# Projecting q with its head columns on partitions, rope pairs as block rows, and weights prepared in half-size units

## The chip, the core and the metric

The kernel runs on one core of a Trainium2 chip. The time is the device time of one execution in microseconds (us); three executions of the kernel before are shown. Everything is computed in float32. A core has a matrix engine (TensorE, PE in the profile), a vector engine (VectorE, DVE), a scalar engine (ScalarE, ACT) and GpSimd (POOL), each running its own instructions in order, and SyncE (SP), which here issues most of the DMA transfers. SBUF is the memory on the chip, with 128 partitions; PSUM holds what TensorE writes, in banks of 512 numbers a partition.

## The reference

One layer of linear attention and one sparse gated feed-forward network, each between a layer norm and a residual. Cut to what matters:

```python
def attention(x, Wq, Wk, Wv, Wo):          # x: (2, 1024, 512); 16 heads of q, 4 of k and v, 128 wide
    q = (x @ Wq.T) ; k = (x @ Wk.T) ; v = (x @ Wv.T)      # split into heads
    q = q * cos + rotate_half(q) * sin     # rope: element d is paired with d + 64 of its head
    k = k * cos + rotate_half(k) * sin
    qf, kf = elu(q) + 1, elu(k) + 1        # four heads of q share one head of k and v
    for each token s: state += kf_s v_s^T ; z += kf_s ; out_s = (qf_s state) / (qf_s z + 1e-6)
    return out @ Wo.T

def ffn(x, w_gate, w_up, w_down):          # 2048 wide
    h = silu(x @ w_gate) * (x @ w_up)
    return keep_2_largest_of_4(h) @ w_down

x = x + layernorm(attention(layernorm(x), ...))
x = x + layernorm(ffn(layernorm(x), ...))
```

## The kernel before, in words

**Strassen products.** All large matrix products are made by one scheme, `strassen` (L109 to L146): the product of two 2x2 block matrices in 7 block products instead of 8, run in the order 1, 2, 6, 5, 7, 4, 3. Each operand comes as seven "factors" (four blocks or their sums; `FACTORS` says which go together). The sums between products are kept apart by PSUM copies on ACT (`keep`, L120) and by additions on DVE (L129, L139, L145); product 7 is added into the bank of which product 6's copy must be done, and so on. Product 4 ends block c21 (handed to `done`), product 3, the last, block c12. `step_input` (L545) makes x's factors from transposed x, `sums` (L412) those of the weights.

**Attention** runs in 16 steps n = 0 to 15: gp = n // 8 is a pass over half of the heads (8 of q, 2 of k and v), c = n % 8 a chunk of 128 tokens of both batches. A step works on the products of k and v (`kv_products`, L611) and of q (`q_products`, L634) for step n + 1, on the four groups of step n, and on the output product of step n - 1 (`o_products`, L747). A group i is one batch and one head of k with its four heads of q:

- `features` (L584): on DVE u = q cos (L592) and r = the rotated half times sin (L598, L599), on POOL u + r (L600), on ACT a relu and an exp (L602, L603), on DVE one last operation (L604). Tokens lie on partitions here, so the rope pair lies within a row. For q's four groups this comes after product 2, at product 4, after product 7's addition and after product 3.
- `q_transposed` (L663): four transposes on TensorE (`transposed`, L528: PSUM pool of two buffers), then an ACT copy to SBUF (L665). `k_transposed` (L629) does the same for k's four.
- `scores` (L668): kT times qT, masked by DVE into `am` (L679).
- `attend` (L684): per head of q one matmul with the state (L697) and one with `am` (L698), of 129 columns (the last column sums z); then, on DVE, the denominators (L703, L704) and o (L706), and the new state (L716, L718).
- `o_transposed` (L733): four transposes of o, an ACT copy for groups 0 to 2 (L738), and for the last group the sums that make the other factors (L741 to L745, one of them on POOL).

A group of q is `(b, j)`, batch and head of k, from `GROUPS` (L609).

**Order.** TensorE's, POOL's and SP's orders are written out by hand (`tc.manual_schedule`, L803); those of DVE and ACT are chosen by a scheduler when the kernel is built, but for the first lines. In each step `first(i)` (L830) issues the transposes ahead of group i, `second(i)` (L844) its attention and the scores of the next; between them parts of the three Strassen runs are advanced, so that TensorE has work while the other engines prepare.

**Start.** The kernel loads x(0), the weights of k and v, of q (L431, in four quarters of 512 columns, 2 KB rows), the rope table (L433), x(1), wo's, x(2), on the queues of ACT and SP. kv(0) and q(0) (the products of step 0) run before any group.

**Weights of later work** are "prepared" by the generator `prepare` (L446): 17 units, each loaded to SBUF (L443), summed by POOL (four operations, L461 to L465) and stored to DRAM as factors (L457, L469). Each call of `first` advances it once; ahead of the units it makes wo's sums (`prepare_all`, L508).

**FFN.** Four blocks of 512 tokens (`hidden` L265, `down` L314) of Strassen products (L218, L324), with the selection of 2 of 4 on DVE and POOL. The first gate products are interleaved with the last attention step.

Of the kernel before, what the change touches and what calls it, by code (L numbers as in the profile page):

```python
# [35 lines left out]
def kernel(  # L36
# [366 lines left out]
    def q_quarter(gp, i, k):  # L403
        return rows(wq, 2 * k, 2, (2 * gp + i) * 512, 512)
# [7 lines left out]
    def sums(t, engine):  # L412
        a11, a12, a22, s2, s4, s3, s1 = (t[:, i] for i in range(7))
        for o, i0, i1, op in (
            (s1, s3, a22, ALU.add),
            (s3, a11, s3, ALU.subtract),
            (s2, s1, a11, ALU.subtract),
            (s4, a12, s2, ALU.subtract),
        ):
            engine.tensor_tensor(o, i0, i1, op)  # L420
            yield

    def load_quarters(t, quarter, engines):
# [7 lines left out]
    load_quarters(wq_sb, q_quarter, (nc.scalar, nc.sync))  # L431
# [5 lines left out]
    xt[2] = load_x(2)  # L437
    weights = {0: (wkv_sb, wq_sb, wo_sb)}

    def prepare_load(src, view, dst):  # L440
        q = prep.tile([P, 4, 512], F32, tag="q", name="wraw")
        for to, of in src(q):
            nc.sync.dma_start(out=to, in_=of)  # L443
        return view(q), dst
# [29 lines left out]
    def whole(of):  # L474
        return lambda q: [(q, of)]

    def quarters(quarter, part):
        def src(q):
            for n, (i, k) in enumerate(((0, 0), (0, 1), (1, 0), (1, 1))):
                of = quarter(1, i, k)[:, part]  # L480
                yield q[:, n, :].rearrange("p (k c) -> p k c", c=of.shape[2]), of

        return src

    def view_quarters(q):
        return [q[:, n, :] for n in range(4)]

    def view_gu(q):
        v = q.rearrange("p (h k) (j m c) -> p h k j m c", h=2, j=2, m=2)
        return [v[:, h, :, :, m, :] for m, h in ((0, 0), (0, 1), (1, 0), (1, 1))]  # L490

    def view_d(q):
        v = q.rearrange("p (h k) (m c) -> p h k m c", h=2, m=2)
        return [v[:, h, :, m, :] for m, h in ((0, 0), (0, 1), (1, 0), (1, 1))]

    def into_gu(t):
        return lambda n: t[:, n, :].rearrange("p (k j c) -> p k j c", k=2, j=2)

    def into_d(jb):
        return lambda n: d_dram[:, n, jb, :].rearrange("p (k c) -> p k c", k=2)  # L500

    def into_part(t, part):
        return lambda n: t[:, n, part]

    def part_of(t, part):
        return lambda n: t[:, n, part].rearrange("p k c -> p (k c)")

    def prepare_all():  # L508
        yield from sums(wo_sb, nc.gpsimd)
        units = []  # L510
        for quarter, t, parts in (
            (kv_quarter, wkv_dram, (slice(0, 2),)),
            (q_quarter, wq_dram, (slice(0, 1), slice(1, 2))),
            (o_quarter, wo_dram, (slice(0, 2), slice(2, 4))),
        ):
            for part in parts:
                units.append((quarters(quarter, part), view_quarters, part_of(t, part)))
        for jb in range(NJB):
            for i, w in enumerate((w_gate, w_up)):
                units.append((whole(columns(w, jb)), view_gu, into_gu(gu_dram[jb][i])))  # L520
        for jb in range(NJB):
            of = w_down[jb * 512 : (jb + 1) * 512, :].rearrange("(p r) o -> p r o", r=4)
            units.append((whole(of), view_d, into_d(jb)))
# [56 lines left out]

    def strassen_a(width, product, c11, c12, c22, done):
        return strassen((ps_mm, qp), [P, width // HD, HD], product, c11, c12, c22, done)

    def features(src, c, dst):  # L584
# [5 lines left out]
        u = rawp.tile([P, 4, HD], F32, tag="u", name="u")  # L590
        r = rawp.tile([P, 4, HD], F32, tag="r", name="r")
# [13 lines left out]

    kf, kT, v1, qf = {}, {}, {}, {}
    GROUPS = ((0, 0), (1, 1), (0, 1), (1, 0))  # L609
# [24 lines left out]
    def q_products(n):  # L634
        c = n % NC
        raw = [rawp.tile([P, REP, HD], F32, tag="raw", name="qraw", bufs=4) for _ in range(3)]

        def feature(i, src):
            f = qp.tile([P, REP, HD], F32, tag="qf", name="qf", bufs=3)
            features(src, c, f)  # L640
            qf[n, i] = f

        run = strassen_a(
            512,
            project(weights[n // NC][1], xf[n]),
            raw[0],
            raw[2],
            raw[1],
            lambda t: feature(2, t),
        )  # L650
        for i, _ in enumerate(run):
            if i == 1:
                feature(0, raw[0])
            elif i == 4:
                feature(1, raw[1])
            elif i == 6:
                feature(3, raw[2])
            yield

    state = {}  # L660
    qT, am, o = {}, {}, {}

    def q_transposed(n, i):  # L663
        t = qp.tile([P, REP, P], F32, tag="qT", name="qT")
        nc.scalar.copy(t, transposed(qf.pop((n, i))))  # L665
        qT[n, i] = t

    def scores(n, i):  # L668
# [5 lines left out]
            qT[n, i].rearrange("p h t -> p (h t)"),  # L674
# [9 lines left out]
    def attend(n, i):  # L684
# [8 lines left out]
        q, a = qT.pop((n, i)), am.pop((n, i))  # L693
        for h in range(REP):
            dst = nmv[:, h // 2, h % 2, :]
            if c > 0:
                nc.tensor.matmul(dst, q[:, h, :], state[b, j], start=True, stop=False)  # L697
# [35 lines left out]
    def o_transposed(n, i):  # L733

        t = transposed(o.pop((n, i)))
        if i < 3:
            place = (0, 2, 1)[i]
            nc.scalar.copy(factor(n, place, 1 if place == 1 else 2), t)  # L738
# [271 lines left out]
```

## Time and profile before

| | |
|---|---|
| median of three executions | 1396.29 us (1395.09, 1396.29, 1398.87) |
| the profiled execution | 1395.51 us |
| its span, first to last instruction | 1393.8 us |
| mean granted TensorE clock | 0.996 |
| first kv product, first q product | 18.9 us, 29.9 us |
| last q product of attention ends, first FFN product starts | 724 us, 772 us |
| DMA: 109732 packets, 197.48 MB | mean 142 GB/s |

The profile comes from a hardware profiler during one execution, so rows are durations in that execution. A row of its groups names the line of the kernel, the engine, the operation, output and input by the program's names, the shape (partitions x elements) and the number; then the total busy time, the mean of one in ns, and the idle time of the engine just before those instructions with what ended it. A row of a timeline gives the start in us, the duration, the engine, line, operation and shape, and in brackets the wait before it and its releaser. A row of the windows gives the stretch, then for PE, weight loads, DVE, ACT and POOL the busy time and the number of instructions, then the granted clock, the DMA share and GB/s. Digits of the slices are busy tenths of 40 equal parts of the span.

### The profile page before, as it was taken

To read this page: it belongs to the slowest core of one execution; us is meant where nothing else is said; L and a number is where in the kernel's file an instruction comes from. 1 tells how busy PE (TensorE), PEld (TensorE's weight loads), DVE (VectorE), ACT (ScalarE), POOL (GpSimd) and SP (SyncE) were. 2 spreads that over 40 slices of the span, in tenths; PEclk is the share of its full clock that TensorE was granted. 3 is DMA by queue.
4 is the path that set the end of the run, shared out by engine and by line. 5 is a ranking of instruction groups with operands and counts; after the bars stand their busy time and mean duration, and the time that the engine had idled before them with its cause. 6 is when DMAs were issued, how large, how long until landed. Compare 5 with 4: busy or idle time off the path is not lost. (4 is left out here: it accounts for less than half of the span.)

```text
span 1393.8 us, 17195 instructions
## 1 busy us (share of the span) xinstructions
PE 1335.9 (96%) x6384; PEld 1069.0 (77%) x6384; DVE 835.1 (60%) x1570; ACT 447.3 (32%) x797; POOL 321.5 (23%) x259
## 2 busy tenths in 40 slices
PE   4899999999999999999999999999999999999997
PEld 2567778777876787667678888888888888888886
DVE  5785766564556565656566439816772577526852
ACT  1543433433233324333342323214330333113210
POOL 0333322332333343444332110100000100110001
PEclk9999999999999999999999999999999999999999
DMA  6131345035841736233443455346544655355321
GB/s 245 42 125 52 105 162 186 28 97 178 274 140 64 242 113 215 82 108 123 153 144 129 128 213 152 116 165 217 152 128 152 222 153 154 117 201 152 91 79 73
DMA packets 109732, 197.48 MB, mean 142 GB/s; under 512 B 8272, under 2 KB 51280, under 8 KB 105552
## 3 DMA queue, kind: packets, MB, share of 16 engines
q1 hardware_dynamic: 107520, 194.02, 43.1%
q10 hardware_dynamic: 2128, 2.36, 0.5%
q8 instruction: 51, 0.84, 0.2%
q14 instruction: 33, 0.27, 0.1%
HBM read 145.23 MB, written 51.12 MB: 141 GB/s over the span
## 5 line engine op out<-in xcount | busy, mean ns | idle before, releaser
L120 ACT COPY u<-cb 128x512 f32<-128x512 f32 (+1 forms) x252 | 126.1, 500 | 474.7 <-PE cb L218 183.1
L600 POOL TENSOR_TENSOR u<-u,r 128x512 f32<-128x512 f32 x80 | 101.8, 1273 | 300.9 <-DVE r L599 190.1
L570 PE MATMUL cb<-wq,xf 128*128 128x512 f32 x256 | 121.3, 596 | 7.0 <-ACT u L120 7.0
L755 PE MATMUL cb<-wo,of 128*128 128x256 f32 x512 | 121.2, 379 | 0.5 <-ACT u L120 0.5
L218 PE MATMUL cb<-fxt,wgu 128*128 128x256 f32 x512 | 117.8, 381 | 1.0 <-ACT u L120 1.0
L218 PE MATMUL cb<-fxnT,wgu 128*128 128x256 f32 x512 | 116.9, 379 | 0.0
L755 PEld LDWEIGHTS cb<-wo,of 128*128 128x128 f32 x512 | 95.9, 190 | 26.3 <-issue 11.9
L218 PEld LDWEIGHTS cb<-fxt,wgu 128*128 128x128 f32 x512 | 96.6, 190 | 16.4 <-ACT u L120 3.6
L218 PEld LDWEIGHTS cb<-fxnT,wgu 128*128 128x128 f32 x512 | 97.1, 190 | 13.8 <-issue 0.5
L604 DVE SCALAR_TENSOR_TENSOR qf<-u,r 128x512 f32<-128x512 f32 x64 | 65.4, 1021 | 66.3 <-ACT r L603 58.4
L168 POOL TENSOR_TENSOR h<-h 128x512 f32<-128x512 f32 x16 | 23.5, 1467 | 331.1 <-DVE ht L165 331.1
L602 ACT ACTIVATE r<-u 128x512 f32<-128x512 f32 x80 | 50.4, 631 | 153.9 <-POOL u L600 153.9
L139 DVE TENSOR_TENSOR y<-u,ce 128x256 f32<-128x256 f32 (+1 forms) x20 | 9.5, 474 | 146.8 <-ACT u L120 146.8
L698 PE MATMUL nm<-v,am 128*128 128x129 f32 x512 | 96.0, 277 | 1.5 <-DVE am L679 1.5
L570 PEld LDWEIGHTS cb<-wq,xf 128*128 128x128 f32 x256 | 46.6, 190 | 55.9 <-issue 40.7
L697 PE MATMUL nm<-state,qT 128*128 128x129 f32 x448 | 86.6, 275 | 0.0
L698 PEld LDWEIGHTS nm<-v,am 128*128 128x128 f32 x512 | 76.8, 194 | 3.4 <-issue 3.3
L697 PEld LDWEIGHTS nm<-state,qT 128*128 128x128 f32 x448 | 71.0, 191 | 7.7 <-issue 6.2
L570 PE MATMUL cb<-wkv,xf 128*128 128x256 f32 x256 | 67.8, 388 | 1.9 <-DVE xf L556 1.4
L671 PE MATMUL sc<-qT,kT 128*128 128x512 f32 x128 | 66.1, 598 | 0.0
L324 PE MATMUL cb<-wd,h 128*128 128x256 f32 x256 | 58.3, 381 | 4.0 <-DVE h L306 3.9
L755 PE MATMUL ce<-wo,of 128*128 128x256 f32 x256 | 60.5, 379 | 0.0
(151 smaller groups left out, 2571.6 us busy)
## 6 DMA issues: line engine op xcount, KB each, us to landing
wgu<-gs SPq DMA_DIRECT2D x112, 256.0 KB, 2.7
wgu<-us SPq DMA_DIRECT2D x112, 256.0 KB, 2.7
wd<-d_dram SPq DMA_DIRECT2D x28, 1024.0 KB, 4.8
xf<-xf SPq DMA_DIRECT2D x16, 896.0 KB, 5.1
x<-in_x_dram SPq DMA_DIRECT2D x16, 512.0 KB, 5.9
gs<-wraw SPq DMA_DIRECT2D x28, 256.0 KB, 3.5
us<-wraw SPq DMA_DIRECT2D x28, 256.0 KB, 3.5
d_dram<-wraw SPq DMA_DIRECT2D x28, 256.0 KB, 2.8
```

What stands on the lines that cost most here:

```text
L120: nc.scalar.copy(t, b)
L168: (engine or nc.gpsimd).tensor_tensor(b12, b22, b12, ALU.subtract)
L218: nc.tensor.matmul(bank[:, j, :], w[:, k, j, :], xf[xi][:, k, :], start=(start and j == 0 and k == 0), stop=(j == 1 and k == 1), skip_grou ...
L324: nc.tensor.matmul(bank[:, j, :], hf[jb][hi][:, k, j * P : (j + 1) * P], w[:, jb, k, :], start=(start and jb == 0 and j == 0 and k == 0), ...
L570: nc.tensor.matmul(bank.rearrange("p h d -> p (h d)"), x_[:, xi, k, :], w[:, wi, k, :], start=(start and k == 0), stop=(k == 1), skip_grou ...
L600: nc.gpsimd.tensor_tensor(u, u, r, ALU.add)
L602: nc.scalar.activation(r, u, AF.Relu, scale=-1.0)
L604: nc.vector.scalar_tensor_tensor(dst, u, 0.0, r, ALU.max, ALU.add)
L671: nc.tensor.matmul(sc.rearrange("p h t -> p (h t)"), kT[n][:, 2 * b + j, :], qT[n, i].rearrange("p h t -> p (h t)"), start=True, stop=True,)
L697: nc.tensor.matmul(dst, q[:, h, :], state[b, j], start=True, stop=False)
L698: nc.tensor.matmul(dst, a[:, h, :], v, start=(c == 0), stop=True)
L755: nc.tensor.matmul(bank.rearrange("p h d -> p (h d)"), of[n, xi][:, k, :], w[:, wi, k, :], start=(start and k == 0), stop=(k == 3), skip_g ...
```

## The change

q is projected with the operands of TensorE exchanged (`project_transposed`): the weights are held, 128 columns at a time, and x's transposed chunk is streamed, so that a product leaves the columns of heads on partitions and 128 tokens along the row, as the scores need them. The 2x2 blocks are now (halves of heads) x (batch): the first block row holds elements 0 to 63 of each of the eight heads, the second 64 to 127, and 128 partitions hold the halves of two heads. So the two members of a rope pair stand in the same place of two blocks, and both are needed before rope can start.

- `q_quarter` picks the interleaved halves of heads, 64 columns (256 B) at a time; the first load of wq becomes eight transfers.
- Rope for q works along tokens, so the tables are transposed once: `transpose_rope`, called between kv(0) and q(0), with four DVE copies, four sets of four transposes on TensorE and four ACT copies.
- `features_transposed` does a batch's two groups at a time: two halves, each with two DVE products, one POOL operation, two ACT operations and two final DVE operations of 64 partitions, which write the halves of a head onto the partitions 0 to 63 and 64 to 127 of `qT`. It is called at product 4 (batch 0) and after product 3 (batch 1). u and r have three buffers instead of two.
- `q_transposed` is gone, with its 64 sets of transposes and ACT copies.
- `GROUPS` goes batch by batch. In `o_transposed` two of the ACT copies remain, one group is written straight as a difference by DVE, and the last by DVE, ACT and POOL.
- The units of the weights that are prepared are half as wide: 34 instead of 17, and `second` advances the generator as well as `first`. wo's sums, ahead of the units, so come one per `first` or `second`.

The diff, cut to its core:

```diff
@@ -401,7 +401,9 @@
         return rows((wk, wv)[i], 2 * k, 2, gp * 256, 256)
     def q_quarter(gp, i, k):
-        return rows(wq, 2 * k, 2, (2 * gp + i) * 512, 512)
+        of = rows(wq, 2 * k, 2, 8 * gp * HD, 8 * HD)
+        return of.rearrange("p k (h i d) -> p k h i d", h=8, i=2)[:, :, :, i, :]
     def o_quarter(gp, i, k):
         return rows(wo, (2 * gp + k) * 4, 4, i * 256, 256)
...
-    load_quarters(wq_sb, q_quarter, (nc.scalar, nc.sync))
+    for k in range(2):
+        for n, (to, i, kh) in enumerate(((0, 0, 0), (1, 0, 1), (5, 1, 0), (2, 1, 1))):
+            (nc.scalar, nc.sync)[n % 2].dma_start(
+                out=wq_sb[:, to, k, :].rearrange("p (h d) -> p h d", h=8),
+                in_=q_quarter(0, i, kh)[:, k],
+            )
...
+    rope_T = [wp.tile([P, S], F32, name=name) for name in ("cos_T", "sin_T")]
+    def transpose_rope():
+        for t, k in zip(rope_T, (0, 2)):
+            for c in range(0, NC, 4):
+                twice = rawp.tile([P, 4, 2, 64], F32, tag="u", name="twice", bufs=3)
+                of = rope_sb[:, c : c + 4, k, :].unsqueeze(2).broadcast_to([P, 4, 2, 64])
+                nc.vector.tensor_copy(twice, of)
+                pt = transposed(twice.rearrange("p c s d -> p c (s d)"))
+                nc.scalar.copy(t[:, c * P : (c + 4) * P].rearrange("p (j t) -> p j t", j=4), pt)
...
-        q = prep.tile([P, 4, 512], F32, tag="q", name="wraw")
+        q = prep.tile([P, 4, 256], F32, tag="q", name="wraw")
...
+        yield from sums(all_of(wo_sb), nc.gpsimd)
+        units = [unit(kv_quarter, k, wkv_dram) for k in range(2)]
+        units += [unit_q(k, n) for k in range(2) for n in range(2)]
+        units += [unit(o_quarter, k, wo_dram) for k in range(4)]
...
+            units += [unit_gu(w, jb, i, j) for i, w in enumerate((w_gate, w_up)) for j in range(2)]
+        units += [unit_d(jb, k) for jb in range(NJB) for k in range(2)]
...
+    def project_transposed(w, x_):
+        def product(bank, i, start):
+            wi, xi = FACTORS[i]
+            for hp in range(4):
+                for k in range(2):
+                    nc.tensor.matmul(
+                        bank[:, hp, :],
+                        w[:, wi, k, hp * P : (hp + 1) * P],
+                        x_[:, xi, k, :],
+                        start=(start and hp == 0 and k == 0),
+                        stop=(hp == 3 and k == 1),
+                        skip_group_check=True,
+                    )
+        return product
...
-        u = rawp.tile([P, 4, HD], F32, tag="u", name="u")
-        r = rawp.tile([P, 4, HD], F32, tag="r", name="r")
+        u = rawp.tile([P, 4, HD], F32, tag="u", name="u", bufs=3)
+        r = rawp.tile([P, 4, HD], F32, tag="r", name="r", bufs=3)
...
+    def features_transposed(lo, hi, c):
+        cos, sin = (
+            t[:, c * P : (c + 1) * P].unsqueeze(1).broadcast_to([P, 4, P]) for t in rope_T
+        )
+        t = qp.tile([P, 4, 2, P], F32, tag="qT", name="qT")
+        for i, (same, other, op) in enumerate(((lo, hi, ALU.subtract), (hi, lo, ALU.add))):
+            u = rawp.tile([P, 4, P], F32, tag="u", name="u", bufs=3)
+            r = rawp.tile([P, 4, P], F32, tag="r", name="r", bufs=3)
+            nc.vector.tensor_tensor(u, same, cos, ALU.mult)
+            nc.vector.tensor_tensor(r, other, sin, ALU.mult)
+            nc.gpsimd.tensor_tensor(u, u, r, op)
+            nc.scalar.activation(r, u, AF.Relu, scale=-1.0)
+            nc.scalar.activation(r, r, AF.Exp, scale=-1.0)
+            for s in range(2):
+                half_of = slice(64 * s, 64 * s + 64)
+                nc.vector.scalar_tensor_tensor(
+                    t[64 * i : 64 * i + 64, :, s, :], u[half_of], 0.0, r[half_of], ALU.max, ALU.add
+                )
+        return t
+    kf, kT, v1, qT = {}, {}, {}, {}
+    GROUPS = ((0, 0), (0, 1), (1, 0), (1, 1))
...
-        raw = [rawp.tile([P, REP, HD], F32, tag="raw", name="qraw", bufs=4) for _ in range(3)]
-        def feature(i, src):
-            f = qp.tile([P, REP, HD], F32, tag="qf", name="qf", bufs=3)
-            features(src, c, f)
-            qf[n, i] = f
-        run = strassen_a(
-            512,
-            project(weights[n // NC][1], xf[n]),
-            raw[0],
-            raw[2],
-            raw[1],
-            lambda t: feature(2, t),
-        )
-        for i, _ in enumerate(run):
-            if i == 1:
-                feature(0, raw[0])
-            elif i == 4:
-                feature(1, raw[1])
-            elif i == 6:
-                feature(3, raw[2])
-            yield
+        raw = [rawp.tile([P, 4, P], F32, tag="raw", name="qraw", bufs=4) for _ in range(3)]
+        def done(hi):
+            qT[n, 0] = features_transposed(raw[0], hi, c)
+        yield from strassen_a(
+            512, project_transposed(weights[n // NC][1], xf[n]), raw[0], raw[1], raw[2], done
+        )
+        qT[n, 1] = features_transposed(raw[1], raw[2], c)
...
-    def q_transposed(n, i):
-        t = qp.tile([P, REP, P], F32, tag="qT", name="qT")
-        nc.scalar.copy(t, transposed(qf.pop((n, i))))
-        qT[n, i] = t
...
-            qT[n, i].rearrange("p h t -> p (h t)"),
+            qT[n, b][:, 2 * j : 2 * j + 2].rearrange("p a s t -> p (a s t)"),
...
-        q, a = qT.pop((n, i)), am.pop((n, i))
+        q, a = qT[n, b], am.pop((n, i))
...
-                nc.tensor.matmul(dst, q[:, h, :], state[b, j], start=True, stop=False)
+                nc.tensor.matmul(dst, q[:, 2 * j + h // 2, h % 2, :], state[b, j], start=True, stop=False)
...
-        if i < 3:
-            place = (0, 2, 1)[i]
-            nc.scalar.copy(factor(n, place, 1 if place == 1 else 2), t)
+        if i < 2:
+            nc.scalar.copy(factor(n, i, 2), t)
+        elif i == 2:
+            nc.vector.tensor_tensor(factor(n, 3, 1), t, of[n, 0], ALU.subtract)
         else:
-            t1, t2, t3, t4 = (factor(n, 3 + k, 1) for k in range(4))
-            nc.vector.tensor_tensor(t1, t, of[n, 0], ALU.subtract)
-            nc.vector.tensor_tensor(t2, of[n, 2], t1, ALU.subtract)
+            b22, t2, t3, t4 = (factor(n, place, 1) for place in (2, 4, 5, 6))
+            nc.vector.tensor_tensor(t2, t, of[n, 3], ALU.subtract)
+            nc.scalar.copy(b22, t)
...
         finish(kv_products(0))
+        transpose_rope()
         qpr = q_products(0)
...
-        q_transposed(0, 0)
...
-                if i < 3:
-                    q_transposed(n, i + 1)
-                elif more:
-                    q_transposed(n + 1, 0)
...
             def second(i):
+                next(preparing, None)
                 attend(n, i)
```

## The prediction

> **What bounds the kernel now.** I read the busy totals first, then the slices, then who waited on whom, then the timelines by engine of one stretch of the middle and of the start.
>
> ```profile
> PE 1335.9 (96%) x6384; PEld 1069.0 (77%) x6384; DVE 835.1 (60%) x1570; ACT 447.3 (32%) x797; POOL 321.5 (23%) x259
> PE   4899999999999999999999999999999999999997
> ```
> TensorE (PE) sets the end: its queue is full in all slices but the first two and the last. Work taken off it shortens the run only where nothing else is late in its place. One step of attention takes about 47.4 us (the kv products start at 280.25 and again at 327.65). TensorE's timeline of such a step:
>
> ```profile
> 301.50 1.88 PE L570 MATMUL cb<-wq,xf 128*128 128x512 f32 x4
> 303.21 1.88 PE L570 MATMUL ce<-wq,xf 128*128 128x512 f32 x4
> 304.93 0.60 PE L532 MATMUL pst<-ident,qf 128*128 128x128 f32 x4
> 305.37 0.60 PE L532 MATMUL pst<-ident,o 128*128 128x128 f32 x4
> 306.20 0.66 PE L532 MATMUL pst<-ident,kf 128*128 128x128 f32 x4 [0.24 <-ACT qT L665]
> ...
> 310.15 0.39 PE L697 MATMUL nm<-state,qT 128*128 128x129 f32 x2
> 310.37 0.39 PE L698 MATMUL nm<-v,am 128*128 128x129 f32 x2
> ```
> Starts matter, not the modelled durations: a q product (two matmuls of 512 columns) costs 1.72 us, four transposes 0.44, a matmul of 129 columns with weights of its own 0.2225, and the third set of transposes in a row waits 0.24 for a PSUM buffer. VectorE (DVE) has slack on average, but it runs in order and shares something with GpSimd (POOL). First line from DVE's timeline, second from POOL's:
>
> ```profile
> 307.94 1.33 DVE L592 TENSOR_TENSOR u<-qraw,rope_sb 128x512 f32<-128x512 f32 x1
> ```
> ```profile
> 307.46 1.27 POOL L600 TENSOR_TENSOR u<-u,r 128x512 f32<-128x512 f32 x1 [3.53 <-DVE r L599]
> ```
> The same DVE operation takes 0.69 when POOL is idle; here it ends 0.54 after POOL's. So a DVE operation with its inputs in SBUF waits for a running POOL operation to end (am and o, which read PSUM, keep their 0.67). And an idle TensorE pays twice:
>
> ```profile
> 83.25 0.65 PE L532 MATMUL pst<-ident,qf 128*128 128x128 f32 x4 [2.64 <-ACT xf L552]
> 84.60 1.90 PE L698 MATMUL nm<-v,am 128*128 128x129 f32 x8
> 86.73 1.67 PE L671 MATMUL sc<-qT,kT 128*128 128x512 f32 x2
> ```
> After 2.64 us idle the eight matmuls take 1.7 instead of 0.9; the granted clock is 0.66 in 84 to 86 us and 0.50 in 86 to 88, a loss of some 2 us. The Trainium skill ("TensorE: Matmul & The Clock Gate", section "What's actually happening") lets the clock fall only after an idle window of about 3.4 us; by it the shorter gaps below would cost their length alone, some 3 us less in the sum. This row decides against it.
>
> **TensorE's own sum.** Gone: 64 sets of q transposes x 0.44 = -28.2. Added: four sets for the rope tables, +1.8. The q products keep their columns, but as 8 matmuls of 128 with weights of their own. Nearest row: 0.2225 x 128/129 = 0.221, so 1.77 a product against 1.72; over 16 x 7 = 112 products +5.6 (from 0, same columns, to +6.7 at 0.2225 each). The waits of 0.24 behind the q copies (5.8 us in all by the table of waits) go: -5. Together -25.8, if nothing else becomes late.
>
> **What becomes late in a step.** q now needs both halves of a pair, so the features start at product 4 (the last but one) instead of after product 2, and the half that lands on each partition half needs its own final operation: 8 per step of 64x512 where 4 of 128x512 were. No row has 64 partitions; cost goes with elements per partition in the rows (256: 0.42, 512: 0.69), so I take the 0.61 from start to start of a 512 row (bounds: 0.3 if partitions counted, 1.02, the qf mean). I lay one step out by these durations, in the order in which the built program lists each engine, from the first q product: product 4 ends at 13.8. r and u from PSUM 13.95 to 15.2; POOL's first add to 15.9, its second 16.5 to 17.8; ScalarE (ACT) does relu and exp (0.65 each) between copies; the first two final operations 17.8 to 19.0, next u and r to 20.25, POOL's third add 20.85 to 22.1, fourth 24.0 to 25.2, its relu and exp to 26.5. Only behind these in ACT's queue stands the PSUM copy that o's product 7 waits for: it ends at 26.95, TensorE is there at 26.2. New wait 0.75 a step (0 without POOL conflicts, 1.5 with one more). Two more: (1) the last transposes of x now wait for a DVE subtraction from the same PSUM buffers instead of an ACT copy, 0.7 in five steps; (2) the second half of q overwrites the buffer that attend(n,3) reads, so four final operations (2.45) run only after it, ahead of that group's division; o is ready 6.2 after attend starts, its transposes come at 6.3: a tie, which a prepared unit's POOL operation (half of 1.27 now) breaks; I take 0.3 (0 to 1.5). Step 1 to 14: -1.75 + 0.38 - 0.24 + 0.75 + 0.3 = -0.56 each, -7.8; + 3.5 for (1); step 15 loses three sets, -1.3. **Sum -6** (-24 with no new wait, +6 with the upper bounds).
>
> **The start.** Four things. (a) The rope chain. Before, q(0) starts when kv(0) ends, at 29.9. Now DVE copies the tables after k's rope operations (32.4), is blocked by POOL's add once, TensorE transposes, ACT copies; between those copies ACT runs k's exp with two table loads of 1.28, and the fourth set needs the second copy (38.0). q(0) starts near 38.4, cold: +8.5 and 2. (b) kv(1): before, 2.0 of wait and 1.7 of cold at 44.9; now its third product waits about 3 for a copy behind q's relu. Equal. (c) In step 0 POOL runs the four wo sums (2.63 each) back to back where they were split in two pairs; two normalizations and k's final operation stand between them on DVE ahead of o(0,0): 0 to 6.6 of wait, I take 3. (d) In step 0 there are no o products to cover the features: from the end of product 4, DVE has 11.8 us of operations (0.61 each, 0.2 the small ones) before o(0,2), TensorE only 5.5 us; a wait of 6.4 bare, 9.6 with POOL conflicts, against 2.85 before: +3.5 to +7. With the transposes saved here (8 x 0.44) and the cold clock after two waits (+2 each): 10.5 + 3 + 5 + 4 - 3.5 - (waits of 2.1 that were there before o(0,0)) = **+17** (+9 to +21); I take +15, as some of the conflicts will not meet.
>
> **The first weights.** q's 2 MB arrive in pieces of 64 columns, 256 B, where they were 2 KB. x(1), which DVE's queue needs before it finishes x(0), lies behind them; the DMA engines are full until 22 us, so a longer load moves everything. In the windows, 2 KB pieces ran at 387 GB/s with the engines busy, 512 B pieces at 286:
>
> ```profile
> 10.00:15.00 5.00, 0.00 (x0) 0.00 (x0) 0.00 (x0) 0.41 (x1) 0.00 (x0) 1.00 1.06 387
> 316.00:317.00 1.00, 1.00 (x6) 0.87 (x6) 0.00 (x0) 0.00 (x0) 0.00 (x0) 1.00 1.05 286
> ```
> That is 90 ns and 30 ns a piece on an engine; a straight line gives 20 ns for 256 B: 8192 pieces / 16 x 20 = 10.2 us against 5.4, +4.8. Bounds: 0 (bytes alone count) and +10 (30 ns, as a piece of 512 B). I take **+4**. "DMA: Bandwidth & Descriptors", section "Why small descriptors are slow (HBM only)", speaks against this edit too: 27% overhead at 256 B, which would be +1.5 here. Half-size units of the other weights move the same bytes in pieces no smaller than 512 B, on queues with idle time, and POOL does twice as many operations of half the width: nothing, unless POOL waits for their DMAs (15 us before); then q's adds behind them are late.
>
> **Sum.** 1395.5 (profiled execution; span 1393.8 and 1.7 around it) - 6 + 15 + 4 = 1408.5; the median of three is 0.8 above that execution. I say 1408.
>
> **Rivals.**
> - A, faster: TensorE's sum gets through, one mechanism: no wait takes the place of the transposes in steps 1 to 15, since all three are ties within a microsecond. Steps -24, start +9, load +2: 1383. It decides where the new waits of a step fall below 0.6 us. For it: TensorE at 96%, DVE at 60%. Against: in-order queues, and POOL's conflicts, which the rows show.
> - B, nothing: waits of 0.3 a step (-14), start +11, load +3: 1395.5.
> - C, worse: the final operations after attend(n,3) meet POOL in most steps, and copies late by 1.5 bring clock drops: steps +8, start +19, load +6: 1428.
> - D, the narrow matmuls don't do what is hoped: 16 weight loads at the 190 ns that a load row shows would make a product 3.0 us, +148, 1543. The rows of 129 columns, with loads of 194 ns at a spacing of 0.1112 a piece, exclude it nearly.
>
> **Numbers.** Forecast (1400 to 1420) 0.60, A 0.14, B 0.13, C 0.12, D 0.01. 0.3% is about what a measurement of this kernel can tell from no change. Faster by more: A, 0.14. Within: B, 0.13. Slower: 0.73. The range reaches from A's upper part to C: 1387 to 1427.
>
> **What would show it.** TensorE's step period after 110 us: 46.8 by the forecast, 45.8 by A. q products at 1.77 apart. q(0) starting near 42 (38.4 and the load's 4); idle TensorE of 6 us and more ahead of the transposes of o in step 0, released by DVE; waits of o's product 7 for an ACT copy, 0.75 in most steps; x(1) landing near 19.7 instead of 15.7. Wrong if the conflicts with POOL fall apart in time, or if 64-partition operations cost half.

## The result

The changed kernel takes 1436.95 us (median of six; 1433.8 to 1437.81) against 1396.05: a ratio of 1.0283 [1.0272, 1.0294], slower by 41 us. The forecast was 1408 in 1387 to 1427: the sign was right, the size was not, and the range did not hold it.

Busy totals of the page after, then its slices for TensorE and for the granted clock:

```profile
PE 1331.4 (93%) x7488; PEld 1165.2 (81%) x7488; DVE 892.2 (62%) x1574; ACT 419.1 (29%) x739; POOL 347.2 (24%) x327
...
PE   2778899989999999999999999999999999999997
...
PEclk9888999999999999999999999999999999999999
```

TensorE is busy for 4.5 us less and the span (1433.4) is 39.6 longer: the loss is waiting, more than half of it in the first five slices (26 of the 44 us that TensorE is idle longer). I cut both spans where the kv products of a step begin. kv(n) are the products that step n needs, and they run in step n - 1; the five stretches from kv(2) to kv(7) are called steps 2 to 6 in what was written ahead of the runs. `e7` and `e16` are runs told below.

| stretch, us | before | after | difference | forecast | e7 | e16 |
|---|---|---|---|---|---|---|
| start to kv(2) | 89.6 | 118.5 | +28.9 | +19 | 109.2 | 97.7 |
| kv(2) to kv(7) | 238.0 | 246.9 | +8.8 | } | 234.0 | 237.8 |
| kv(7) to kv(15) | 371.6 | 374.1 | +2.4 | } -6 | 359.0 | 367.8 |
| kv(15) to the end | 694.5 | 694.0 | -0.5 | } | 693.4 | 696.6 |

**A step.** TensorE's timeline after, from the same stretch of work that the forecast showed:

```profile
288.82 1.95 PE L611 MATMUL cb<-xf,wq 128*128 128x128 f32 x16
290.61 1.95 PE L611 MATMUL ce<-xf,wq 128*128 128x128 f32 x16
292.40 0.60 PE L556 MATMUL pst<-ident,o 128*128 128x128 f32 x4
...
304.30 1.96 PE L800 MATMUL cb<-wo,of 128*128 128x256 f32 x8 [1.09 <-ACT u L120]
...
307.79 0.66 PE L556 MATMUL pst<-ident,x 128*128 128x128 f32 x4 [0.65 <-DVE of L783]
...
316.82 0.63 PE L556 MATMUL pst<-ident,o 128*128 128x128 f32 x4 [2.06 <-DVE o L750]
```

A q product costs 1.79 (forecast 1.77), q's transposes are gone, and three waits have come: 1.09 for the copy ahead of o's product 7, 0.65 for the difference that holds a PSUM buffer, 2.06 for the last group's o. The whole list of TensorE's waits (total, times, longest):

```profile
PE pst L556 <- DVE o L750: 25.5, 13, 11.0
PE pst L556 <- DVE x L107: 22.5, 2, 15.2
PE cb L800 <- ACT u L120: 15.4, 14, 2.2
```

DVE's timeline ahead of that o, then POOL's of the same time:

```profile
310.22 4.11 DVE L664 SCALAR_TENSOR_TENSOR qT<-u,r 64x512 f32<-64x512 f32 x4
314.34 0.85 DVE L582 TENSOR_TENSOR xf<-xf 128x256 f32<-128x256 f32 x1
315.12 0.15 DVE L747 TENSOR_SCALAR den<-nm 128x4 f32<-128x4 f32 x1
315.19 0.68 DVE L723 TENSOR_TENSOR am<-sc,causal 128x512 f32<-128x512 f32 x1
315.79 0.16 DVE L748 RECIPROCAL den<-den 128x4 f32<-128x4 f32 x1
315.99 0.69 DVE L750 TENSOR_TENSOR o<-nm,den 128x512 f32<-128x512 f32 x1
```
```profile
310.79 0.72 POOL L484 TENSOR_TENSOR wraw<-wraw 128x256 f32<-128x256 f32 x1 [5.11 <-DMA gs<-wraw]
311.59 1.06 POOL L485 TENSOR_TENSOR wraw<-wraw 128x256 f32<-128x256 f32 x1
312.73 1.05 POOL L487 TENSOR_TENSOR wraw<-wraw 128x256 f32<-128x256 f32 x1
313.86 1.05 POOL L488 TENSOR_TENSOR wraw<-wraw 128x256 f32<-128x256 f32 x1
```

The attention's last matmul starts at 310.1, but o is made at 316: ahead of it on DVE stand four final operations of q, and a prepared unit's four POOL operations fall between them. Two steps earlier no unit meets them, and the same four take 2.78 (wait 0.29):

```profile
212.57 2.78 DVE L664 SCALAR_TENSOR_TENSOR qT<-u,r 64x512 f32<-64x512 f32 x4
```

**Step 0.** TensorE's two largest waits of the attention, then POOL's wo sums and the two DVE rows that they held; with POOL idle these rows take 1.1 (two operations) and 0.7:

```profile
87.67 1.11 PE L556 MATMUL pst<-ident,o 128*128 128x128 f32 x4 [4.50 <-DVE o L750]
88.58 3.62 PE L611 MATMUL cb<-xf,wq 128*128 128x128 f32 x16
...
113.47 1.09 PE L556 MATMUL pst<-ident,o 128*128 128x128 f32 x4 [11.02 <-DVE o L750]
```
```profile
77.83 10.53 POOL L423 TENSOR_TENSOR wo<-wo 128x1024 f32<-128x1024 f32 x4
```
```profile
79.13 4.28 DVE L107 TENSOR_SCALAR x<-x,mv,rs 128x512 f32<-128x512 f32 x2
83.33 2.82 DVE L645 SCALAR_TENSOR_TENSOR kf<-u,r 128x512 f32<-128x512 f32 x1
```

After the first of these waits a q product takes 3.4 us from start to start instead of 1.79.

**The first loads.** The first statistics of x(1) start at 21.35, before at 15.7. In the windows the DMA engines are busy at 218 GB/s, where the forecast showed 387:

```profile
8.00:12.00 4.00, 0.00 (x0) 0.00 (x0) 0.00 (x0) 0.00 (x0) 0.00 (x0) 1.00 1.35 218
```

### The profile page after: what moved, and what is told of

It is laid out like the page before. It is cut to its first block, busy times and chain, and to the rows that moved or that the text cites. A ratio compares the mean times of both kernels' runs of the same rounds, so it can differ in the third digit from the quotient of the medians.

```text
span 1433.4 us, 19682 instructions
## 1 busy us (share of the span) xinstructions
PE 1331.4 (93%) x7488; PEld 1165.2 (81%) x7488; DVE 892.2 (62%) x1574; ACT 419.1 (29%) x739; POOL 347.2 (24%) x327
## 5 line engine op out<-in xcount | busy, mean ns | idle before, releaser
L659 POOL TENSOR_TENSOR u<-u,r 128x512 f32<-128x512 f32 x64 | 88.5, 1383 | 226.5 <-DVE r L658 217.6
L611 PEld LDWEIGHTS cb<-xf,wq 128*128 128x128 f32 x1024 | 125.1, 196 | 11.1 <-issue 7.6
L611 PE MATMUL cb<-xf,wq 128*128 128x128 f32 x1024 | 128.6, 280 | 1.7 <-ACT u L120 1.6
L664 DVE SCALAR_TENSOR_TENSOR qT<-u,r 64x512 f32<-64x512 f32 x128 | 119.1, 930 | 11.7 <-ACT r L661 5.5
L660 ACT ACTIVATE r<-u 128x512 f32<-128x512 f32 x64 | 40.3, 630 | 163.8 <-POOL u L659 160.8
L594 PEld LDWEIGHTS cb<-wkv,xf 128*128 128x128 f32 x256 | 47.1, 195 | 25.5 <-ACT u L120 12.2
L556 PE MATMUL pst<-ident,o 128*128 128x128 f32 x256 | 40.1, 280 | 25.6 <-DVE o L750 25.5
```

The lines of the kernel that those rows point to most:

```text
L556: nc.tensor.transpose(t[:, j, :], src[:, j, :], ident)
L594: nc.tensor.matmul(bank.rearrange("p h d -> p (h d)"), x_[:, xi, k, :], w[:, wi, k, :], start=(start and k == 0), stop=(k == 1), skip_grou ...
L611: nc.tensor.matmul(bank[:, hp, :], w[:, wi, k, hp * P : (hp + 1) * P], x_[:, xi, k, :], start=(start and hp == 0 and k == 0), stop=(hp == ...
L659: nc.gpsimd.tensor_tensor(u, u, r, op)
L660: nc.scalar.activation(r, u, AF.Relu, scale=-1.0)
L664: nc.vector.scalar_tensor_tensor(t[64 * i : 64 * i + 64, :, s, :], u[half_of], 0.0, r[half_of], ALU.max, ALU.add)
```

## The experiments

Two theories stood after the result. **T:** VectorE's queue is late, because it does q's final operation twice for 64 partitions each, and POOL's operations block it. **R:** the features come at the wrong time or place (product 4, the buffer of qT, the start), and the operations themselves are covered. The first group of runs takes one thing away each, or puts one into the kernel before; the second keeps the whole computation and takes the double operation away. Ratios are to the kernel before on the same chip, with their 95% intervals, which are 1.5 to 4 us to either side; "less" and "more" compare medians with the changed kernel's 1436.95, if nothing else is said. In the diffs "..." marks what is left out.

### One thing at a time

**e1: a third buffer for qT.**
```diff
-        t = qp.tile([P, 4, 2, P], F32, tag="qT", name="qT")
+        t = qp.tile([P, 4, 2, P], F32, tag="qT", name="qT", bufs=3)
...
-        y = ap_.tile([P, B, DM], F32, tag="y", name="y", bufs=2)
+        y = ap_.tile([P, B, DM], F32, tag="y", name="y", bufs=1)
```


> The changed kernel with three buffers for qT instead of two (y gets one instead of two, for the room). Theory: the final operations of q's second half run late only because their buffer is read by the last group's attention; then o's division stands behind four of them, and POOL's prepared weights stretch them to 4.1 us. With a third buffer they leave the place ahead of that division: the waits of o's transposes at the step's end (2.1, 0.3, 1.65, 2.1, 0.3 us in steps 2 to 6, 2.8 us in all later) go, 9 us: 1427. Rival: the lateness is VectorE's load against POOL's operations, not the buffer; the same operations then stand ahead of the copy that o's product 7 waits for, that wait grows from 1.1 by as much, and the time stays at 1436.

1438.92, 1.0295 [1.0269, 1.0321]: nothing won; my expectation was wrong and its rival right. Its waits:

```profile
PE pst L556 <- DVE o L750: 24.9, 16, 11.0
PE pst L556 <- DVE x L107: 22.6, 2, 15.2
PE cb L800 <- ACT u L120: 19.2, 14, 2.3
```
From kv(2) to kv(7) the waits for o fall to 0.4 to 0.8, those for the copy rise from 1.09 to 1.39. The final operations left their place and were as late in another.

**e2: wq in 2 KB rows.**
```diff
-        "wq": given["L0_attn_Wq"].T,
+        "wq": given["L0_attn_Wq"].T.reshape(DM, 2, 8, 2, 64).transpose(0, 1, 3, 2, 4).reshape(DM, H * HD),
...
-        of = rows(wq, 2 * k, 2, 8 * gp * HD, 8 * HD)
+        of = rows(wq, 2 * k, 2, (2 * gp + i) * 512, 512)
```


> The changed kernel with wq's columns laid out in DRAM in the order in which the kernel wants them, so that the same eight transfers read 2 KB rows instead of pieces of 256 B. Theory: the small pieces hold x(1) back (its statistics start at 21.35 us, 15.7 before), and all of the start with it: 5.6 us less, 1431; ScalarE's four issues of some 2 us each shrink too. Rival: the first kv product waits for x(0), whose square root stands behind ScalarE's issues, and the issues cost by transfer, not by piece: 1435 or more. Second rival: the start is long enough behind (rope chain) to hide it: 1436.

1431.39, 1.0239 [1.0211, 1.0267]: 5.5 less. x(1)'s statistics start at 17.92, kv(0) at 21.1 instead of 24.5, with the engines at 378 GB/s in 8 to 12 us. The Trainium skill's 27% for pieces of 256 B ("DMA: Bandwidth & Descriptors", section "Why small descriptors are slow (HBM only)") is below what these windows show, 378 against 218 GB/s, or 73% more time for the same bytes. The rest up to before's 18.9 stays. ScalarE's first operation stands behind its queue's four transfers of wq, which are issued over 5.7 us (8.2 with the small pieces; before, two in 1.1); that the number of transfers is the cause is argued from these rows, no run has two of them with wide rows.

**e3: rope tables loaded as they are needed.**
```diff
-        transpose_rope()
...
+    for n in range(2):
+        nc.sync.dma_start(out=rope_T[n], in_=ropet[n])
```


> The changed kernel with the transposed rope tables loaded from DRAM (1 MB more, ahead of wo) instead of made by DVE copies, TensorE transposes and ScalarE copies; the rest as it is. Theory: q(0) starts when kv(0) ends, some 8.6 us earlier, and TensorE stays warm, 2.2 more: 1425. Rival: q's features wait for the normalization of x(1) and the queue of VectorE anyway, and step 0's waits take back what is won: 1432 or more.

1424.71, 1.0197 [1.0173, 1.0221]: 12.2 less. q(0) starts at 36.4 instead of 44.1; kv(1) at 50.0 instead of 59.8. The theory holds, and little of it is taken back later: in the profiled execution, the longest of the four, 9.8 us of gain at kv(1) are 10.4 at kv(2) and 7.7 at the end.

**e4: wo's sums once per group in step 0.**
```diff
             def second(i):
-                next(preparing, None)
+                if n > 0:
+                    next(preparing, None)
```


> The changed kernel with the weights' generator advanced once per group in step 0, as before the change, instead of twice, so that wo's four sums come apart in step 0; later steps as changed. Theory: the 10.5 us of sums in a row on POOL block two normalizations and k's final operation on VectorE (4.3 and 2.8 us for them, the first o's transposes wait 4.5 us, cold after it): 4.5 and 1.8 go, 1430. Rival: the 11 us wait further down in step 0, which is VectorE's features of q(1), starts from the same place whatever happens ahead, and takes all of it back: 1436.

1431.48, 1.0243 [1.022, 1.0266]: 5.5 less, but not as expected. In step 0 the first wait falls from 4.5 to 2.4 and the second grows from 11.0 to 13.5; kv(2) starts only 1.8 earlier. In the profiled execution 0.9 more come from there to kv(7) and 1.9 from there to kv(15). The units meet other operations in these steps, but the waits for o from kv(2) to kv(7) (0.3, 1.7, 2.1, 0.3, 2.0) have the sum that they had, 6.4, so which wait gave the rest is not shown.

**e5: q's rope addition on VectorE.**
```diff
-            nc.gpsimd.tensor_tensor(u, u, r, op)
+            nc.vector.tensor_tensor(u, u, r, op)
```


> The changed kernel with q's rope addition (four a step, 1.27 us each on POOL, of 128x512) on VectorE, which does such an operation in 0.61. Theory: what is late in a step is VectorE's chain from product 4 to o, stretched by POOL operations that it may not overlap; each POOL addition costs VectorE 0.7 and the chain 1.3. Without them the waits for o and for product 7's copy shrink by a half or more, in step 0 too: 1425. Rival: VectorE is late by its own load (62% busy), and 0.61 more for each half makes it later: 1445.

1426.23, 1.0196 [1.0174, 1.0217]: 10.7 less, though DVE has 64 operations more. From kv(2) to kv(7) o's wait is 0.3 throughout, step 0's long wait 7.15 instead of 11.0. So POOL's blocking is a part of the lateness, and it costs more than the work that replaces it.

**e6: prepared sums left out.**
```diff
-            nc.gpsimd.tensor_tensor(a22, a21, a22, ALU.add)
-            nc.gpsimd.tensor_tensor(a21, a11, a21, ALU.subtract)
...
-            nc.gpsimd.tensor_tensor(a11, a22, a11, ALU.subtract)
-            nc.gpsimd.tensor_tensor(a12, a12, a11, ALU.subtract)
```


> The changed kernel without POOL's four additions for each prepared unit (their loads and stores stay; the weights of the second pass and of the FFN are then wrong). Theory that the prepared units' operations are what stretches the final operations ahead of o (4.1 us for four in a step where they met, 2.8 where they did not): the waits of 2 us for o in half of the steps go to 0.3, and the clock drops behind them: 1426. Rival: the final operations themselves and q's own POOL additions make it late; the waits stay: 1434.

1422.06, 1.0172 [1.0151, 1.0192]: 14.9 less. o's wait is 0.3 from kv(2) to kv(7), product 7's stays at 1.09. The theory's 1426 was a little high.

**e7: one final operation.**
```diff
-            for s in range(2):
-                half_of = slice(64 * s, 64 * s + 64)
-                nc.vector.scalar_tensor_tensor(
-                    t[64 * i : 64 * i + 64, :, s, :], u[half_of], 0.0, r[half_of], ALU.max, ALU.add
-                )
+            nc.vector.scalar_tensor_tensor(t[:, :, i, :], u, 0.0, r, ALU.max, ALU.add)
```


> The changed kernel with one final operation of 128x512 for each half of q in place of two of 64x512 (the halves of heads are then not brought to their places, so q is wrong). It prices the split: 4 x 0.61 us of VectorE in each step. Theory: this is the largest part of what made VectorE late; product 7's wait (1.1), o's waits (0.3 to 2.1) and 2.4 of step 0's 11 go: 1405 to 1410. Rival: the order (features only at product 4) and POOL's additions make it late: 1428.

1398.0, 1.0003 [0.9991, 1.0014]: 39 less, the time of the kernel before. That is nearly all of the time of the operations taken away (16 steps x 4 x 0.70 from start to start = 45). The table above shows it in all stretches but the last (9.3 in the start, 12.9 and 15.1 in the next two). The waits for o and for product 7's copy have left the head of the list, and the steps from kv(4) to kv(7) take 46.3:

```profile
PE pst L556 <- DVE x L107: 22.5, 2, 15.1
PE cb L594 <- ACT u L120: 8.2, 8, 2.6
PE pst L556 <- ACT xf L579: 5.9, 1, 5.9
```
It is T's largest part, larger than I expected. For the steps R falls, since place and time of the features are the same here and the loss is gone; for the start R stands, which is still 19.6 us longer than before (e2 and e3 show of what).

**e8: the kernel before without q's transposes.**
```diff
-        nc.scalar.copy(t, transposed(qf.pop((n, i))))
+        nc.scalar.copy(t, qf.pop((n, i)))
```


> The kernel before, with q's 64 sets of transposes left out: ScalarE copies q's features straight, untransposed (so the scores are wrong). It prices what the change could have won on TensorE. Theory: 64 x 0.44 us of work and the 5 us of waits behind the copies go, nothing else is late: 1363. Rival: the transposes covered other waits (the features of q, o), which appear now: 1380.

1376.82, 0.9845 [0.9823, 0.9866]: 19.8 less than the kernel before, where 33 were written. The rival's guess was near: behind the transposes stood waits that now appear, for o in step 0 (3.8 and 1.7) and, in the second pass, of q's products for a copy (2.7 instead of 2.0). From TensorE's waits, the first line of before, then two of e8:

```profile
PE cb L570 <- ACT u L120: 7.5, 6, 2.0
```
```profile
PE cb L570 <- ACT u L120: 12.6, 8, 2.7
PE pst L532 <- DVE o L706: 7.2, 4, 3.8
```
The gain depends on the stretch: 9.7 us from kv(2) to kv(7), where 8.8 of transposes are left out; 10.5 from kv(7) to kv(15), where 14.1 are; and none in step 0, whose stretch from kv(1) to kv(2) takes 45.8 us, before 45.7. The gain that the change could have was smaller than TensorE's sum said.

**e12: half-size units in the kernel before.**
```diff
-        q = prep.tile([P, 4, 512], F32, tag="q", name="wraw")
+        q = prep.tile([P, 4, 256], F32, tag="q", name="wraw")
...
             def second(i):
+                next(preparing, None)
```


> The kernel before with the prepared units of half size and two advances of their generator a group, and nothing else of the change. Theory: same bytes, same time on POOL, and VectorE in that kernel has the slack to be blocked: 1397, at most 2 more for wo's sums in a row in step 0. Rival: operations on POOL that meet VectorE's in each group cost what they cost in the changed kernel (14 us without them there): 1405 or more.

1395.49, 0.999 [0.9979, 1.0002]: no difference. Units of half size, and twice as many of them, cost nothing in the kernel before. What the sums themselves cost there was not measured, as e6 leaves them out of the changed kernel only.

### The whole computation with one final operation

A DMA can bring the halves of heads to their partitions, so that one final operation is enough.

**e9: halves by DMA.**
```diff
...
+            nc.vector.scalar_tensor_tensor(r, u, 0.0, r, ALU.max, ALU.add)
+            for s in range(2):
+                nc.sync.dma_start(out=t[64 * i : 64 * i + 64, s], in_=r[64 * s : 64 * s + 64])
```


> The changed kernel with one final operation of 128x512 for each half of q, written in place, and the halves of heads brought to their partitions of qT by four DMAs for each batch (128 KB each, on SP's queue); qT has three buffers, y one. The result is the reference's. Theory, from the run with one final operation (1398): TensorE needs the features some 10 us after they are made, so that a transfer of 2 to 3 us is hidden, and the price of the split goes: 1398 to 1402. Rival: SP's queue stands waiting for the final operations, the prepared weights behind it come late to POOL and meet other operations, or scores wait for the transfer: 1415 or more.

1481.61, 1.0608 [1.0587, 1.0629]: the rival, and worse than it said. SP's own waits name it: in order behind the transfers stand the loads of x's factors, for which kv products then wait (6.3 us at kv(8)).

```profile
SPq L664 <- DVE r L662: 245.2, 48, 21.0
```

**e10** adds e2, e3 and e4 to e9; **e11** adds e5 too.


> The run with halves placed by DMA, and with it the three edits of the start: wq's columns in the kernel's order in DRAM (5.5 us measured alone), rope tables loaded transposed (12.2), wo's sums one per group in step 0 (5.5, of which about half in step 0). If the start's losses add up: 1378. Rival: they overlap, each stands in for the next: 1388.

1475.57, 1.0565 [1.0538, 1.0591].


> The run before this one, and q's rope addition on VectorE instead of POOL (10.7 us measured alone with the split final operations). With half of the final operations gone, VectorE has fewer operations that POOL can block, so about a third of it: 1374. Rival: VectorE's own load (0.61 more for each half) now counts and cancels it: 1380.

1432.89, 1.0262 [1.0238, 1.0286]. Both expectations fail on the same queue, whose wait for the final operations is 255 and 253 us. In e11 the first pass is what was hoped (kv(2) at 89.1, five steps of 46.25), and the second loses it, with q's products waiting 5 to 10 us for ScalarE's copies. The timelines lead from the longest of these waits (9.9, ended at 533.5) back to that queue: ScalarE's copy stands behind k's exp, this behind POOL's addition, and POOL had waited for the transfer of a prepared unit, whose place is behind the halves on SP's queue:

```profile
513.17 0.72 POOL L477 TENSOR_TENSOR wraw<-wraw 128x256 f32<-128x256 f32 x1 [22.48 <-DMA gs<-wraw]
```

**e13: the transfers issued later.**
```diff
             def first(i):
...
+                if i == 3:
+                    place_halves(n + 1, 0)
+                elif i == 0:
+                    place_halves(n, 1)
```


> The changed kernel with one final operation for each half, and the halves placed by DMAs that are issued late (batch 0's ahead of the step's last group, batch 1's at the next step's start), so that SP's queue does not stand before them; r has five buffers, y one, qT two. Theory: VectorE's extra 2.45 us a step are the price; 1398, as with the values left wrong. Rival: features are needed at once, and the transfers (2.3 us from issue to landing) show as waits of the scores: 1415 or more.

1462.55, 1.047 [1.0444, 1.0497]: neither theory. The transfers are short, but they now stand behind stores of prepared weights, and those wait for POOL (247 us of SP's time). TensorE's list:

```profile
PE sc L727 <- DMA qT<-r: 43.0, 8, 9.2
```

**e14** is e13 with e2, e3 and e4, **e15** with e5 too.


> The same, with wq's columns in the kernel's order in DRAM, the rope tables loaded transposed, and wo's sums one per group in step 0. If the start's losses (5.5, 12.2 and 5.5 us alone) add up: 1376. Rival: the start is bound by VectorE's queue in step 0, and they give half: 1387.

1450.63, 1.0386 [1.0364, 1.0409].


> The same, with q's rope addition on VectorE. The earlier run with the blocked queue had steps of 46.25 us and no wait but 0.65 in its first pass. Theory: 1372. Rival: VectorE's 0.61 more a half is late in the second pass, where y's normalization comes to VectorE: 1380.

1397.91, 1.0011 [1.0, 1.0022]; two waits for transfers are left, 6.0 and 6.9 us.

**e16: e2, e3, e4 and e5 together, the final operations split.**


> The changed kernel with the split final operations as they are, and the three start edits and the rope addition on VectorE. Theory: alone they gave 5.5, 12.2, 5.5 and 10.7 us; the price of the split stays, some of the step 0 terms overlap: 1405. Rival: without POOL's blocking the split costs little: 1390.

1400.42, 1.0029 [1.002, 1.0039]: 36.5 less than the changed kernel, where the four alone gave 33.9 in sum. Within their intervals they add up. Still, o's wait of 7.2 in step 0 and some of the copy's are left.

**e17** is e11, **e18** is e15, with the transfers on ScalarE's queue.
```diff
-                nc.sync.dma_start(out=t[64 * i : 64 * i + 64, s], in_=r[64 * s : 64 * s + 64])
+                nc.scalar.dma_start(out=t[64 * i : 64 * i + 64, s], in_=r[64 * s : 64 * s + 64])
```


> The run with halves placed by DMA as soon as they are made, the three start edits and the rope addition on VectorE, but with the transfers issued by ScalarE's queue instead of SP's (where x's factors and the second pass's weights stood behind them). Theory: steps of 46.25 us in the first pass stay, and the second pass's waits of 7 to 10 us go: 1375. Rival: ScalarE stands before the transfers' inputs and its PSUM copy for o's product 7 comes late by the issue and the wait, 1 to 2 us a step: 1395.

1431.87, 1.0256 [1.0228, 1.0285]: issued at once, they hold ScalarE before its copies, and o's product 7 waits 31 us in all.


> The run with late transfers, the three start edits and the rope addition on VectorE (1398, two waits of scores for transfers, 6.0 and 6.9 us), with the transfers issued by ScalarE's queue. Theory: both waits go, 1385 or a little less. Rival: issues on ScalarE delay its copies, 1395.

1392.72, 0.9965 [0.9954, 0.9976]: faster than both kernels, by 4 and 44 us; no wait of the scores for a transfer is left, but 8 us more than I expected. In step 0 a wait for o of 4.5 has come, nearly as long as the 6.0 that went (e15 has only the other one, of 4.0), and ScalarE's copies are waited for, 2.5 and 2.7 us at the longest:

```profile
PE pst L549 <- DVE o L755: 8.9, 3, 4.5
```

## Why the prediction went wrong

- **Where the miss lies.** By the forecast's terms the four stretches of the table should have changed by +19, +0.7 (five steps, with the 3.5 of (1)), -4.5 (eight steps) and -1.9. They changed by +28.9, +8.8, +2.4 and -0.5. So 9.9 us were missed in the start, 8.1 from kv(2) to kv(7) and 6.9 from there to kv(15). Of the 8.1, o's wait is 4.9, the copy's 1.7, and the cold clock after one of the waits 1.6. In the 6.9 the waits ahead of product 7 (0.96 to 2.15) are 3.5 above the 0.75 taken. In e8 the transposes of that stretch gave 3.6 less than their time, which would fit the rest; but that is the other kernel, so this part is not shown.
- **The final operations.** "Cost goes with elements per partition" was right: 64x512 takes 0.69, as 128x512 does, and 0.70 from start to start with POOL idle (0.61 written). The step that failed is what they do to VectorE's queue: **"I take 0.3 (0 to 1.5)"** for o behind four of them, and the +5 taken for o(0,2) in step 0. The first measured 2.1, 0.3, 1.65, 2.1 and 0.3 from kv(2) to kv(7), 1.3 on average: within its bounds, but 1 us a step above the value in the sum. The second is in the item on step 0. I had named what breaks the tie, a prepared unit, and priced it as one POOL operation; it is four, in three of these five steps, and stretches 2.78 us of DVE work to 3.74 to 4.62. Taken away, half of the final operations give 39 us back (e7), where the sum had only new waits, of about 1 us a step, and step 0's 5.
- **TensorE's sum** was right in its rows (1.79 against 1.77 a product; 0.44 for four transposes) and wrong as a gain: the kernel before without the transposes gains 20, not 33. Other waits stood behind them and took the rest.
- **The copy ahead of product 7** waits 1.09 for 0.75, the PSUM buffer 0.65 for 0.7: these two of the step's three new waits were laid out by hand to within 0.4 us, the third, o's, was not.
- **Step 0** is the larger part of the start's miss. From q(1) to kv(2) it takes 46.3 us, before 34.6: +11.7 where (c), (d), the cold clock and what was saved came to 6.4 (3 + 5 + 4 - 3.5 - 2.1), and I took off 2 because "some of the conflicts will not meet". They met: the wait for o(0,2) was 11.0 where it had been 2.85, above the 9.6 with conflicts, and wo's sums cost 4.5 and a cold q product. The 3.5 credited for step 0's transposes is not seen in e8, where leaving them out saves nothing in that step. e4 shows that the two are one thing: with the sums apart, the second wait grows by what the first loses.
- **The rope chain** was right: q(0) starts 14.2 later, 5.7 of it the load and 8.5 the chain (8.5 written), and the cold clock takes some 2 more; e3 gives it back whole. **The load** was 5.7 for 4, within its bounds; e2 gives 3.4 of it back at kv(0); the rest I put down to the number of transfers, which is not shown. kv(1) to q(1) is 1.3 longer instead of equal.
- **Half-size units** cost nothing by themselves (e12, in the kernel before), as written. Where DVE is late, the units' sums cost 15 us (e6), which was not foreseen; whether units of full size would cost less there was not tried.
- **Rivals.** C (steps +8, start +19, load +6) named the mechanism of the steps, with 0.12. Measured are +10.7 for the steps and +28.9 for start and load, past both. A needed new waits under 0.6 a step: where DVE is relieved (e11), steps take 46.25 with one wait of 0.65.
- **Two slips in the sums** change little: the 0.8 us between the profiled execution and the median is named and then left out (1409.3, not 1408), and 2 KB at 387 GB/s over 16 engines is 85 ns a piece, not 90.

What stays open: that the split costs 39 us rests on e7, which leaves the placing of the halves out. With the placing done the price is not one number: with POOL's additions gone and the start mended, e16 and e18 differ by 8, and e18's transfers cost something of their own. The split, POOL's blocking and the sums of wo share the same lost slack, so that what each one costs depends on which others are there.

## What to carry to other kernels

When work is taken from the engine that is full and put on one that is 60% busy, lay out the second engine's queue between two things that the first waits for, and ask whether any operation more fits there; here four, 2.8 us a step, did not, and the run without them gave 39 us back. A DMA that takes such work over needs a queue in which nothing ahead of it waits for a slow engine, and a place in the order at which its input is ready; on SP's queue, with no other edit, it made the changed kernel 26 to 45 us slower; on ScalarE's, issued late, it beat the split operations (e16, the same other edits) by 8. Price a gain by leaving the work out of the kernel before: that gave 20 where the sum said 33.

## What the runs showed of the hardware

A short idle stretch can halve TensorE's clock for a few us, and does not always. After 2.11 us the next products took 1.7 us each instead of 0.86; after 2.06 us (at 316.82 above) they did not. The length alone does not decide it in this range: in e2 2.02 us were enough (granted clock 0.63 in 313 to 317 us), in e4 2.12 us were not (1.00 in 264 to 268 us). The Trainium skill ("TensorE: Matmul & The Clock Gate", section "What's actually happening") has a window of about 3.4 us that runs freely, which would fit the chance, but not so short an idle time; the rows decide. TensorE's timeline after, and the window with its granted clock of 0.57:

```profile
167.88 0.73 PE L556 MATMUL pst<-ident,o 128*128 128x128 f32 x4 [2.11 <-DVE o L750]
168.40 1.91 PE L594 MATMUL cb<-wkv,xf 128*128 128x256 f32 x4
170.11 1.81 PE L594 MATMUL ca<-wkv,xf 128*128 128x256 f32 x4
```
```profile
168.00:172.00 4.00, 4.00 (x14) 3.32 (x14) 1.64 (x3) 0.96 (x2) 1.81 (x2) 0.57 1.06 278
```

Blocking between VectorE and POOL works both ways: while the four final operations ran, three of POOL's four operations of 128x256 took 1.05 each instead of the 0.73 that they take alone.
